# Two-layer graph network on one core: a cell's products with x computed during the pass over adj and kept in DRAM

## The chip, the core and the metric

The kernel runs on one core of a Trainium2 chip. The metric is the device time of one execution in microseconds; lower is better. Before the change it is 1171.91 us, the median of three runs (1171.31 to 1177.44). The profile is one separate execution of the same program; its span is 1052.2 us. PE stands for TensorE, DVE for VectorE, ACT for ScalarE, POOL for GpSimd, SP for SyncE.

## The reference, cut to what matters

`x` is 2708 x 256, `adj` is a sparse 2708 x 2708 matrix, both float32. Layer 0 sends two "supports" through two gated cells; layer 1 is an attention layer over the entries of adj above 0.5. Both end in a residual and a layer norm.

```python
def _gru_cell(x, hstate, Wih, Whh, bih, bhh):
    gi = x @ Wih.T + bih
    gh = hstate @ Whh.T + bhh          # hstate is x, the layer's input
    ir, iz, inn = jnp.split(gi, 3, axis=1)
    hr, hz, hn = jnp.split(gh, 3, axis=1)
    r = jax.nn.sigmoid(ir + hr)
    z = jax.nn.sigmoid(iz + hz)
    n = jnp.tanh(inn + r * hn)
    return (1.0 - z) * n + z * hstate

# layer 0
node_support = node_adj_norm @ h                       # adj without its diagonal
edge_output = _gru_cell(node_support, h, edge_Wih, edge_Whh, edge_bih, edge_bhh)
edge_support = (sum of three attention heads over the nonzeros of adj) / 3
node_output = _gru_cell(edge_support, h, node_Wih, node_Whh, node_bih, node_bhh)
x = layernorm(x + de[:, None] * edge_output + dn[:, None] * node_output)
# layer 1: four heads over adj > 0.5, then layernorm(x + ...)
```

The products `hstate @ Whh.T` depend on x and weights alone. The products with `Wih` need the supports, and those need adj.

## The kernel before

All work is on one core, in three stages.

1. **The pass over adj.** Columns of the transposed adj are taken in six groups of up to 512 (the last has 148), each in 22 blocks of 128 rows (the last has 20). For each block ScalarE makes two masks, VectorE a maximum over 64 columns at a time, and TensorE adds up flags and attention logits. After each group, `listed` turns what was found into lists of row numbers for the gathers.
2. **Layer 0.** GpSimd gathers the listed rows of adj and of a table `T0` in DRAM; TensorE multiplies them. When the columns of a group are complete, `cells_and_norm` runs the two cells for it and writes its part of layer 1's table `T1`.
3. **Layer 1.** Rows of `T1` are gathered and multiplied in the same way.

The kernel's operations are not issued in the order of the text. A class `Plan` records them with their dependences and a rough time each, and issues them in an order of its own: each engine takes next, of what is ready, the operation with the longest chain of work after it. So the text gives the dependences and not the order.

```python
def issue(self):                                     # Plan
    ...
        if op.method == "dma_start":
            moved = max(moved, t + self.LOAD) + done - self.LOAD
            end = moved
            free[e] = max(free[e], moved - self.LOAD - self.QUEUED)
```

PSUM has eight banks of 128 x 512 float32; five rings share them:

```python
accs, dbs = banks("acc", 2), banks("db", 2)
acc_bank, db_bank = ring(accs), ring(dbs)
side, pl_bank, ls_bank = ring(banks("side", 2)), ring(banks("pl", 1)), ring(banks("ls", 1))
```

The pass, for each group `g` and block `b` (eight tiles `at`, four each of `over` and `mask`):

```python
for g, cs in enumerate(groups):
    w = width[g]
    pe, pf = acc_bank(), db_bank()
    for b in range(NB):
        ...                                          # group 0: loads of xT, small products; later: one other load
        at = tiles.tile([P, CH], F32, name="at")
        nc.sync.dma_start(at[:p, :w], adjT[b * P : b * P + p, base[g] : base[g] + w])
        over = tiles.tile([P, CH], BF16, name="over", bufs=4)
        nc.scalar.activation(over[:p, :w], at[:p, :w], AF.Sign, bias=minus_half[:p])
        ...                                          # GpSimd: the diagonal block loses its diagonal
        mask = tiles.tile([P, CH], BF16, name="mask", bufs=4)
        nc.scalar.activation(mask[:p, :w], at[:p, :w], AF.Sign)
        nc.vector.tensor_reduce(found0[...], at[...], AX.X, ALU.max, apply_absolute_value=True)
        ...
        nc.tensor.matmul(pf[:NB, :w], lhsT=only[:p, b, :], rhs=over[:p, :w], ...)
        nc.tensor.matmul(pe[:H3, :w], lhsT=u3[:p, b, :], rhs=mask[:p, :w], ...)
    logits(g, pe)                                    # copies pe on ScalarE
    flags(g, pf)                                     # reads pf on VectorE
    ...
    listed(0, *ranked[0][g])
```

The cells of a group (two cells `n`, two halves `o` of the 256 outputs, three gates; `w_h` is W_hh, `w_i` is W_ih; KD is 2):

```python
def product(gate, terms):
    pg = side()
    todo = [(wt, v, k) for wt, v in terms for k in range(KD)]
    for m, (wt, v, k) in enumerate(todo):
        nc.tensor.matmul(pg[:, :w], lhsT=wt[:, k, r0 : r0 + P], rhs=v[k], ...)
    return pg[:, :w]

r, zt, t = (gp.tile([P, CH], F32, name=f"g_{v}")[:, :w] for v in "rzt")     # two buffers each
both = ((w_h, of_x), (w_i, of_s))
nc.scalar.activation(r, product(0, both), AF.Sigmoid, bias=bias(b_s, 0))
nc.scalar.activation(zt, product(1, both), AF.Sigmoid, bias=bias(b_s, 1))
nc.vector.scalar_tensor_tensor(t, product(2, both[:1]), bias(b_h, 2), r, op0=ALU.add, op1=ALU.mult)
nc.vector.tensor_add(t, t, product(2, both[1:]))
nc.scalar.activation(t, t, AF.Tanh, bias=bias(b_i, 2))
...                                                  # VectorE: (x - t) * z + t, and the sum of the cells
```

A slower general path for inputs that don't fit the lists stands behind the fast one; it isn't taken for this input.

Of the kernel before, what the change touches and what calls it, by code (L numbers as in the profile page):

```python
# [94 lines left out]
class Plan:  # L95
# [118 lines left out]
    def issue(self):  # L214
        ops, total = self.ops, len(self.ops)
        after = [[] for _ in ops]
        for n, op in enumerate(ops):
            for k in op.deps:
                after[k].append(n)
        tail, urgent = [0.0] * total, [op.urgent for op in ops]  # L220
        for n in reversed(range(total)):
            op = ops[n]
            for m in after[n]:
                tail[n] = max(tail[n], tail[m] + (0.0 if ops[m].engine == op.engine else self.LAG))
                urgent[n] = max(urgent[n], urgent[m])
            tail[n] += op.done
        tail = [t + u for t, u in zip(tail, urgent)]
        left = [len(op.deps) for op in ops]
        start = [0.0] * total
        free = dict.fromkeys(self.ENGINES, 0.0)  # L230
        ready = {e: [] for e in self.ENGINES}
        for n, op in enumerate(ops):
            if not left[n]:
                ready[op.engine].append(n)
        moved, table = 0.0, 0
        for _ in range(total):
            t, e = min((max(free[e], min(start[n] for n in ready[e])), e) for e in self.ENGINES if ready[e])
            n = max((n for n in ready[e] if start[n] <= t), key=lambda n: (tail[n], -n))
            ready[e].remove(n)
            op = ops[n]  # L240
            busy, done = op.busy, op.done
            if op.table and op.table != table:
                busy, done, table = busy + 1.3, done + 1.3, op.table
            free[e] = t + busy
            end = t + done
            if op.method == "dma_start":
                moved = max(moved, t + self.LOAD) + done - self.LOAD
                end = moved
                free[e] = max(free[e], moved - self.LOAD - self.QUEUED)
            for call in op.calls:  # L250
                call()
            for m in after[n]:
                same = ops[m].engine == e and "dma" not in op.method
                start[m] = max(start[m], end + (0.0 if same else self.LAG))
                left[m] -= 1
                if not left[m]:
                    ready[ops[m].engine].append(m)
        return max(free.values())
# [32 lines left out]
def fast_path(ctx: ExitStack, tc: tile.TileContext, i: dict, out: bass.AP, bad: bass.AP):  # L291
# [43 lines left out]
    def ring(tiles):  # L335

        return cycle(tiles).__next__
# [13 lines left out]
    T1 = dram.tile([N, TW], F32, name="f_T1")  # L351

    TS = dram.tile([NG, HEADS1, CH], F32, name="f_TS")
    plan.pitch = {T0.tensor.name: TW, T1.tensor.name: TW, TS.tensor.name: HEADS1 * CH}


    home1 = const.tile([P, 12 * CH], F32, name="f_home1")
# [214 lines left out]
    def spread(layer, cs, rows, row, place):  # L572

        n, slots = len(cs), ROWS // rows
        T = max((TILES0, TILES1)[layer][c] for c in cs)
        lhs = lists.tile([P, NB, 2 * ROWS], BF16, name="ids")
        ids = lhs.rearrange("p b (m v k) -> p v b m k", m=slots, v=2)[:, :, :, :n]
        shape = [P, NB, n, rows]
        nc.vector.tensor_tensor(
# [112 lines left out]
    def later_kd(src, wide, name):  # L692
        t = const.tile([P, KD, wide], F32, name=name)
        later(t, src.rearrange("(k p) n -> p k n", p=P))
        return t

    for b in range(0, NF, 7):
        e = min(b + 7, NF)
        later(xn[:, b:e, :], x[b * P : e * P, :].rearrange("(b p) d -> p b d", p=P))
    if NF < NB:  # L700
        later(xn[: size[NF], NF, :], x[NF * P :, :])
    cells = []
    for cell in ("edge", "node"):
        w_i = later_kd(i[f"L0_gnn_{cell}_WihT"], 3 * D, f"f_{cell}_wi")
        w_h = later_kd(i[f"L0_gnn_{cell}_WhhT"], 3 * D, f"f_{cell}_wh")
# [75 lines left out]
    def flags(g, pf):  # L781
# [14 lines left out]
        if full < len(bl):  # L796
            p = size[last]
            nc.vector.tensor_copy(flags1[:p, :, last:], v[:p, :, full:])

    for g, cs in enumerate(groups):  # L800
        w = width[g]
        pe, pf = acc_bank(), db_bank()
        c0, nf = base[g] // W0, w // W0
        for b in range(NB):
            p = size[b]
            if g == 0 and b % GR == 0:
                load_xT(b // GR)
                projected_u(b // GR)
            elif g > 0 and loads and b % 2:
                loads.pop(0)()  # L810
            at = tiles.tile([P, CH], F32, name="at")
            nc.sync.dma_start(at[:p, :w], adjT[b * P : b * P + p, base[g] : base[g] + w])
            over = tiles.tile([P, CH], BF16, name="over", bufs=4)
            nc.scalar.activation(over[:p, :w], at[:p, :w], AF.Sign, bias=minus_half[:p])
            if b in cs:
                o = b * P - base[g]
                nc.gpsimd.tensor_mul(at[:p, o : o + p], at[:p, o : o + p], off_diag[:p, :p])
            mask = tiles.tile([P, CH], BF16, name="mask", bufs=4)
            nc.scalar.activation(mask[:p, :w], at[:p, :w], AF.Sign)
            nc.vector.tensor_reduce(  # L820
                found0[:p, c0 : c0 + nf, b], at[:p, : nf * W0].rearrange("p (c i) -> p c i", i=W0), AX.X, ALU.max,
                apply_absolute_value=True,
            )
            if nf * W0 < w:
                nc.vector.tensor_reduce(
                    found0[:p, c0 + nf : c0 + nf + 1, b], at[:p, nf * W0 : w], AX.X, ALU.max,
                    apply_absolute_value=True,
                )
            nc.tensor.matmul(
                pf[:NB, :w], lhsT=only[:p, b, :], rhs=over[:p, :w], start=(b == 0), stop=(b == last)  # L830
            )
            nc.tensor.matmul(
                pe[:H3, :w], lhsT=u3[:p, b, :], rhs=mask[:p, :w], start=(b == 0), stop=(b == last)
            )
# [151 lines left out]
    def cells_and_norm(g):  # L986
# [20 lines left out]
        for n, (w_i, w_h, b_i, b_h, b_s) in enumerate(cells):  # L1007
            of_s = [(sa, es)[n][:, o, :w] for o in range(KD)]
            for o in range(KD):

                def product(gate, terms):
                    pg = side()
                    r0 = gate * D + o * P
                    todo = [(wt, v, k) for wt, v in terms for k in range(KD)]
                    for m, (wt, v, k) in enumerate(todo):
                        nc.tensor.matmul(
                            pg[:, :w], lhsT=wt[:, k, r0 : r0 + P], rhs=v[k],
                            start=(m == 0), stop=(m == len(todo) - 1),
                        )
                    return pg[:, :w]  # L1020

                def bias(t, gate):
                    return t[:, gate * KD + o : gate * KD + o + 1]

                r, zt, t = (gp.tile([P, CH], F32, name=f"g_{v}")[:, :w] for v in "rzt")
                both = ((w_h, of_x), (w_i, of_s))
                nc.scalar.activation(r, product(0, both), AF.Sigmoid, bias=bias(b_s, 0))
                nc.scalar.activation(zt, product(1, both), AF.Sigmoid, bias=bias(b_s, 1))
                nc.vector.scalar_tensor_tensor(
                    t, product(2, both[:1]), bias(b_h, 2), r, op0=ALU.add, op1=ALU.mult  # L1030
                )
# [681 lines left out]
```

## Time and profile before

| | us | share of the span | instructions |
|---|---|---|---|
| span of the profiled execution | 1052.2 | | 13904 |
| TensorE matmul busy | 859.4 | 82% | 3867 |
| VectorE busy | 658.2 | 63% | 2097 |
| GpSimd busy | 566.1 | 54% | 613 |
| TensorE weight load busy | 521.6 | 50% | 3867 |
| ScalarE busy | 505.7 | 48% | 1487 |

The DMA engines moved 106.76 MB in the span. A busy share over the whole span is a mean over the three stages, which use the engines quite differently, so the page also cuts the span into 40 equal slices and gives for each slice and engine the busy share in tenths (9 is 90% or more), the clock that TensorE was granted, and the share of the DMA engines. Groups of instructions are named by engine, operation and the tiles written and read; nearly all have the same line number, that of the class that records operations, so tiles tell them apart. The tiles of the pass have the name `f_home`, of which they are parts.

### The profile page before, as it was taken

The numbers are of one execution on the slowest core, as the hardware profiler recorded it, in microseconds if no ns is written. First come the engines' busy times: TensorE is split into PE (matmuls) and PEld (weight loads), VectorE is DVE, ScalarE is ACT, GpSimd is POOL, SyncE is SP. The second block draws the span as 40 slices with busy tenths as digits, with TensorE's granted clock in tenths as the row PEclk, the third lists the DMA queues.
The fourth block names the chain that finished last, engine by engine and source line by source line (L and its number), as shares of the span: only waits on it lengthen the run. The fifth ranks groups of instructions, "written<-read, shape, count | busy, mean of one in ns | idle before, by whom it ended". The sixth has DMA issues, their size and how long they took to land. (4 is left out here: it accounts for less than half of the span.)

```text
span 1052.2 us, 13904 instructions
## 1 busy us (share of the span) xinstructions
PE 859.4 (82%) x3867; PEld 521.6 (50%) x3867; DVE 658.2 (63%) x2097; ACT 505.7 (48%) x1487; POOL 566.1 (54%) x613
## 2 busy tenths in 40 slices
PE   4867777888779988899998989999999858768860
PEld 4423223666544446553564446446645746766650
DVE  5598698845543869624562467137525558769996
ACT  3799999676542426631473238316623420002251
POOL 2003700577877857777777777724400028787720
PEclk9986667799859989899999999999999979889985
DMA  8688985233221113221233123211300114444413
GB/s 287 184 279 250 287 252 147 52 105 88 58 71 41 35 34 90 73 72 50 66 96 116 43 68 91 62 33 53 96 0 2 49 41 112 146 126 140 112 42 109
DMA packets 71437, 106.76 MB, mean 101 GB/s; under 512 B 20792, under 2 KB 42560, under 8 KB 70712
## 3 DMA queue, kind: packets, MB, share of 16 engines
q1 hardware_dynamic: 50104, 58.63, 18.0%
q0 software_dynamic: 20320, 45.59, 16.6%
q10 hardware_dynamic: 928, 1.57, 0.4%
q8 instruction: 33, 0.54, 0.2%
q14 instruction: 52, 0.43, 0.1%
HBM read 97.21 MB, written 8.54 MB: 101 GB/s over the span
## 5 line engine op out<-in xcount | busy, mean ns | idle before, releaser
L203 POOL DMA_INDIRECT rows<-f_T,f_idx x254 | 293.7, 1156 | 217.2 <-DMA f_T<-f_home 106.4
L203 PE MATMUL acc<-four,rows 128*128 128x256 f32 (+1 forms) x712 | 202.0, 419 | 22.3 <-ACT four L203 20.0
L203 POOL DMA_INDIRECT f_home<-in_adjT_dram,f_idx x163 | 164.7, 1010 | 92.7 <-issue 32.8
L203 ACT ACTIVATE four<-four,rows 128x64 f32<-128x64 f32 (+1 forms) x534 | 145.0, 336 | 65.6 <-DMA rows<-f_T,f_idx 32.9
L203 PEld LDWEIGHTS acc<-four,rows 128*128 128x128 f32 x712 | 133.7, 202 | 58.7 <-ACT four L203 30.3
L203 DVE SCALAR_TENSOR_TENSOR f_home<-f_home,rows,f_m 128x128 f32<-128x128 f32 (+1 forms) x364 | 100.1, 343 | 27.3 <-DMA rows<-f_T,f_idx 23.2
L203 POOL DMA_INDIRECT raw<-in_adj_dram,f_idx x91 | 88.6, 974 | 29.5 <-issue 12.8
L203 ACT ACTIVATE f_home<-f_home,f_minus_half 128x512 bf16<-128x512 f32 (+3 forms) x132 | 85.6, 657 | 13.0 <-PE db L203 12.0
L203 PE MATMUL acc<-f_home,rows 128*65 128x128 f32 (+1 forms) x480 | 70.6, 304 | 21.8 <-DVE f_home L203 20.7
L203 DVE TENSOR_REDUCE f_found<-f_home 128x8 f32<-128x512 f32 (+4 forms) x154 | 76.6, 544 | 5.0 <-POOL f_home L203 4.4
L203 ACT ACTIVATE f_home<-f_home 128x512 bf16<-128x512 f32 (+2 forms) x132 | 73.4, 564 | 9.1 <-PE acc L203 6.7
L203 PE MATMUL db<-f_home,f_only 128*22 128x512 bf16 (+2 forms) x132 | 60.6, 506 | 18.8 <-ACT f_home L203 18.2
L203 PEld LDWEIGHTS acc<-f_home,rows 128*65 128x65 f32 x480 | 57.5, 152 | 32.7 <-DVE f_home L203 25.7
L203 PE MATMUL side<-f_xT,f_edge_wh 128*128 128x512 f32 (+1 forms) x144 | 65.2, 577 | 4.4 <-DVE f_home L203 4.2
L203 POOL TENSOR_TENSOR f_home<-f_home,f_off_diag 128x128 f32<-128x128 f32 (+1 forms) x22 | 11.5, 530 | 101.6 <-ACT f_home L203 88.3
L203 PE MATMUL acc<-f_home,f_home 128*9 128x512 bf16 (+2 forms) x132 | 60.5, 506 | 5.3 <-ACT f_home L203 3.6
L203 PE MATMUL side<-f_xT,f_node_wh 128*128 128x512 f32 (+1 forms) x144 | 62.3, 556 | 2.3 <-DVE f_home L203 2.3
L203 DVE SCALAR_TENSOR_TENSOR four<-f_iota,f_rel,f_home 128x64 f32<-128x64 f32 (+1 forms) x163 | 43.9, 276 | 32.0 <-DMA f_home<-in_adjT_dram,f_idx 11.7
L203 PE MATMUL side<-f_home,f_gat_w 128*128 128x512 f32 (+1 forms) x144 | 60.1, 576 | 4.2 <-DVE f_home L203 4.1
L203 PE MATMUL side<-f_home,f_node_wi 128*128 128x512 f32 (+1 forms) x144 | 62.5, 557 | 0.1
L203 DVE TENSOR_SCALAR f_m<-raw 128x128 uint8<-128x128 f32 (+1 forms) x91 | 22.0, 251 | 64.0 <-DMA raw<-in_adj_dram,f_idx 64.0
L203 PE MATMUL side<-f_home,f_edge_wi 128*128 128x512 f32 (+1 forms) x144 | 62.0, 553 | 0.0
(185 smaller groups left out, 1319.1 us busy)
## 6 DMA issues: line engine op xcount, KB each, us to landing
f_home<-in_adjT_dram SPq DMA_DIRECT2D x105, 256.0 KB, 3.4
f_home<-f_TS SPq DMA_DIRECT2D x5, 1024.0 KB
rows<-f_T SPq DMA_DIRECT2D x31, 132.0 KB, 2.4
rows<-f_T,f_idx POOLq DMA_INDIRECT x254, 2.8
f_T<-f_home SPq DMA_DIRECT2D x21, 132.0 KB, 1.7
f_xn<-in_x_dram SPq DMA_DIRECT2D x3, 896.0 KB
f_T<-f_xn SPq DMA_DIRECT2D x3, 896.0 KB, 6.5
out_dram<-f_xn SPq DMA_DIRECT2D x21, 128.0 KB, 2.0
```

The costliest lines, as they stand in the source:

```text
L203: call = lambda: f(*args, **kwargs)
```

## The change

For the first four of the six groups, the cells' products with W_hh are computed during the pass over adj and written to a DRAM tensor `XH` (48 tiles of 128 x 512 float32, 256 KB each); `cells_and_norm` reads them back. The aim is to move TensorE's work to a stage in which it has more room. To make place for it the pass handles two blocks of adj in one instruction of ScalarE and VectorE. What goes with it:

- the pass uses one pair of PSUM accumulators, and the other pair takes the kept products
- W_hh is loaded first, in group 0 of the pass
- a kept product goes through a ScalarE copy and is sent by a DMA from ScalarE's queue
- the tile `ids` of the lists has one buffer instead of two
- the planner no longer holds back engines other than sync for the DMA queue

```diff
             if op.method == "dma_start":
                 moved = max(moved, t + self.LOAD) + done - self.LOAD
                 end = moved
-                free[e] = max(free[e], moved - self.LOAD - self.QUEUED)
+                if e == "sync":
+                    free[e] = max(free[e], moved - self.LOAD - self.QUEUED)
...
+    KEPT = 4
+    XH = dram.tile([KEPT * 2 * KD * 3 * P, CH], F32, name="f_XH")
...
-        lhs = lists.tile([P, NB, 2 * ROWS], BF16, name="ids")
+        lhs = lists.tile([P, NB, 2 * ROWS], BF16, name="ids", bufs=1)
...
+    kept_bank = ring([accs[1], dbs[1]])
+    keptp = Rings(const, 2)
+    def keep(g, n, o, gate):
+        pg = kept_bank()
+        for k in range(KD):
+            nc.tensor.matmul(
+                pg[:, : width[g]], lhsT=w_hs[n][:, k, gate * D + o * P : gate * D + (o + 1) * P],
+                rhs=xT[:, k, base[g] : base[g] + width[g]], start=(k == 0), stop=(k == KD - 1),
+            )
+        t = keptp.tile([P, CH], F32, name="kept")[:, : width[g]]
+        nc.scalar.copy(t, pg[:, : width[g]])
+        nc.scalar.dma_start(place_kept(g, n, o, gate), t)
...
-        pe, pf = acc_bank(), db_bank()
+        pe, pf = accs[0], dbs[0]
-        for b in range(NB):
+        for b0 in range(0, NB, 2):
+            pair = [b0, b0 + 1]
+            at2 = tiles.tile([P, 2, CH], F32, name="at", bufs=4)
+            over2 = tiles.tile([P, 2, CH], BF16, name="over", bufs=2)
+            mask2 = tiles.tile([P, 2, CH], BF16, name="mask", bufs=2)
...
+            for _ in range(1 if g < 2 else 2):
+                if g > 0 and keeps:
+                    keep(*keeps.pop(0))
+            whole = size[b0 + 1] == P
+            if whole:
+                rows_of = adjT[b0 * P : (b0 + 2) * P, ...].rearrange("(s p) n -> p s n", p=P)
+                nc.sync.dma_start(at2[:, :, :w], rows_of)
...
+            for p, s in parts:
+                nc.scalar.activation(over2[:p, s, :w], at2[:p, s, :w], AF.Sign, bias=minus_half[:p])
...
+                nc.scalar.activation(mask2[:p, s, :w], at2[:p, s, :w], AF.Sign)
...
-                nc.scalar.activation(r, product(0, both), AF.Sigmoid, bias=bias(b_s, 0))
-                nc.scalar.activation(zt, product(1, both), AF.Sigmoid, bias=bias(b_s, 1))
-                nc.vector.scalar_tensor_tensor(
-                    t, product(2, both[:1]), bias(b_h, 2), r, op0=ALU.add, op1=ALU.mult
-                )
+                if g < KEPT:
+                    for gate, v in enumerate((r, zt, t)):
+                        nc.sync.dma_start(v, place_kept(g, n, o, gate))
+                    for gate, v in enumerate((r, zt)):
+                        nc.vector.tensor_add(v, v, product(gate, both[1:]))
+                        nc.scalar.activation(v, v, AF.Sigmoid, bias=bias(b_s, gate))
+                    of_h = t
+                else:
+                    ...                              # as before
+                nc.vector.scalar_tensor_tensor(t, of_h, bias(b_h, 2), r, op0=ALU.add, op1=ALU.mult)
```

A last pair of blocks, 128 and 20 rows, stays in two instructions.

More of the change, by code (lines that the diff above doesn't have):

```diff
@@ L353, in fast_path @@
     TS = dram.tile([NG, HEADS1, CH], F32, name="f_TS")
-    plan.pitch = {T0.tensor.name: TW, T1.tensor.name: TW, TS.tensor.name: HEADS1 * CH}
+    KEPT = 4
+    XH = dram.tile([KEPT * 2 * KD * 3 * P, CH], F32, name="f_XH")
+    plan.pitch = {XH.tensor.name: CH, T0.tensor.name: TW, T1.tensor.name: TW, TS.tensor.name: HEADS1 * CH}
     home1 = const.tile([P, 12 * CH], F32, name="f_home1")
@@ L695, in later_kd @@
         return t
+    cells = []
+    of_cells = ("edge", "node")
+    w_hs = [later_kd(i[f"L0_gnn_{cell}_WhhT"], 3 * D, f"f_{cell}_wh") for cell in of_cells]
     for b in range(0, NF, 7):
@@ L701, in fast_path @@
         later(xn[: size[NF], NF, :], x[NF * P :, :])
-    cells = []
-    for cell in ("edge", "node"):
+    for cell, w_h in zip(of_cells, w_hs):
         w_i = later_kd(i[f"L0_gnn_{cell}_WihT"], 3 * D, f"f_{cell}_wi")
-        w_h = later_kd(i[f"L0_gnn_{cell}_WhhT"], 3 * D, f"f_{cell}_wh")
         b_i = const.tile([P, 3 * KD], F32, name=f"f_{cell}_bi")
@@ L798, in flags, with place_kept @@
             nc.vector.tensor_copy(flags1[:p, :, last:], v[:p, :, full:])
+    kept_bank = ring([accs[1], dbs[1]])
+    keptp = Rings(const, 2)
+    def place_kept(g, n, o, gate):
+        at = (((g * 2 + n) * KD + o) * 3 + gate) * P
+        return XH[at : at + P, : width[g]]
+    def keep(g, n, o, gate):
[8 more added lines that the diff above has]
+        nc.scalar.dma_start(place_kept(g, n, o, gate), t)
@@ L800, in fast_path @@
+    keeps = [
+        (g, n, o, gate) for g in range(KEPT) for n in range(2) for o in range(KD) for gate in range(3)
+    ]
     for g, cs in enumerate(groups):
         w = width[g]
-        pe, pf = acc_bank(), db_bank()
+        pe, pf = accs[0], dbs[0]
         c0, nf = base[g] // W0, w // W0
-        for b in range(NB):
[L805 to L809, printed above, removed]
-                loads.pop(0)()
[L811 to L822, printed above, removed]
-            )
-            if nf * W0 < w:
@@ new lines, in fast_path @@
+        for b0 in range(0, NB, 2):
[3 more added lines that the diff above has]
+            mask2 = tiles.tile([P, 2, CH], BF16, name="mask", bufs=2)
+            for b in pair:
+                if g == 0 and b % GR == 0:
+                    load_xT(b // GR)
+                    projected_u(b // GR)
+            if loads and (g > 0 or b0 in (10, 16)):
+                loads.pop(0)()
+            for _ in range(1 if g < 2 else 2):
[3 more added lines that the diff above has]
+            if whole:
+                rows_of = adjT[b0 * P : (b0 + 2) * P, base[g] : base[g] + w].rearrange("(s p) n -> p s n", p=P)
+                nc.sync.dma_start(at2[:, :, :w], rows_of)
+            else:
+                for b in pair:
+                    nc.sync.dma_start(
+                        at2[: size[b], b - b0, :w], adjT[b * P : b * P + size[b], base[g] : base[g] + w]
+                    )
+            parts = [(P, slice(0, 2))] if whole else [(size[b], slice(b - b0, b - b0 + 1)) for b in pair]
+            for p, s in parts:
+                nc.scalar.activation(over2[:p, s, :w], at2[:p, s, :w], AF.Sign, bias=minus_half[:p])
+            for b in pair:
+                if b in cs:
+                    p, o = size[b], b * P - base[g]
+                    v = at2[:p, b - b0, o : o + p]
+                    nc.gpsimd.tensor_mul(v, v, off_diag[:p, :p])
+            for p, s in parts:
+                nc.scalar.activation(mask2[:p, s, :w], at2[:p, s, :w], AF.Sign)
+                b1, b2 = b0 + s.start, b0 + s.stop
@@ L825, in fast_path @@
                 nc.vector.tensor_reduce(
-                    found0[:p, c0 + nf : c0 + nf + 1, b], at[:p, nf * W0 : w], AX.X, ALU.max,
+                    found0[:p, c0 : c0 + nf, b1:b2].rearrange("p c b -> p b c"),
+                    at2[:p, s, : nf * W0].rearrange("p b (c i) -> p b c i", i=W0), AX.X, ALU.max,
                     apply_absolute_value=True,
                 )
-            nc.tensor.matmul(
-                pf[:NB, :w], lhsT=only[:p, b, :], rhs=over[:p, :w], start=(b == 0), stop=(b == last)
-            )
@@ L832, in fast_path @@
-            nc.tensor.matmul(
-                pe[:H3, :w], lhsT=u3[:p, b, :], rhs=mask[:p, :w], start=(b == 0), stop=(b == last)
-            )
+                if nf * W0 < w:
+                    nc.vector.tensor_reduce(
+                        found0[:p, c0 + nf : c0 + nf + 1, b1:b2].rearrange("p c b -> p b c"),
+                        at2[:p, s, nf * W0 : w].rearrange("p b (c i) -> p b c i", c=1), AX.X, ALU.max,
+                        apply_absolute_value=True,
+                    )
+            for b in pair:
+                p = size[b]
+                nc.tensor.matmul(
+                    pf[:NB, :w], lhsT=only[:p, b, :], rhs=over2[:p, b - b0, :w], start=(b == 0), stop=(b == last)
+                )
@@ L835, in fast_path @@
+            for b in pair:
+                p = size[b]
+                nc.tensor.matmul(
+                    pe[:H3, :w], lhsT=u3[:p, b, :], rhs=mask2[:p, b - b0, :w], start=(b == 0), stop=(b == last)
+                )
         logits(g, pe)
@@ L1026, in cells_and_norm @@
                 both = ((w_h, of_x), (w_i, of_s))
-                nc.scalar.activation(r, product(0, both), AF.Sigmoid, bias=bias(b_s, 0))
-                nc.scalar.activation(zt, product(1, both), AF.Sigmoid, bias=bias(b_s, 1))
-                nc.vector.scalar_tensor_tensor(
-                    t, product(2, both[:1]), bias(b_h, 2), r, op0=ALU.add, op1=ALU.mult
-                )
+                if g < KEPT:
[5 more added lines that the diff above has]
+                    of_h = t
+                else:
+                    nc.scalar.activation(r, product(0, both), AF.Sigmoid, bias=bias(b_s, 0))
+                    nc.scalar.activation(zt, product(1, both), AF.Sigmoid, bias=bias(b_s, 1))
+                    of_h = product(2, both[:1])
+                nc.vector.scalar_tensor_tensor(t, of_h, bias(b_h, 2), r, op0=ALU.add, op1=ALU.mult)
                 nc.vector.tensor_add(t, t, product(2, both[1:]))
```

## The prediction

> **What bounds the kernel now.** I read the head of the page and the 40 slices first, to cut the span into stages; then the busy time of each engine by stage; then the costliest groups; last the instructions in order of time, because a mean duration is not the spacing at which instructions of one kind follow each other.
>
> ```profile
> span 1052.2 us, 13904 instructions
> ...
> PE   4867777888779988899998989999999858768860
> ...
> DVE  5598698845543869624562467137525558769996
> ACT  3799999676542426631473238316623420002251
> ...
> PEclk9986667799859989899999999999999979889985
> DMA  8688985233221113221233123211300114444413
> ```
>
> A slice is 26.3 us. Slices 1 to 7 (to about 190 us) are the pass over adj: DMA at 8 or 9, ACT at 9, PE at 7 on a clock of only 6 to 8 tenths. Slices 8 to 32 (to about 850 us) are layer 0's gathers with the cells between them: PE at 9, DMA at 1 to 3. The last 200 us are layer 1, where DVE is highest. The busy times by stage put numbers on it (columns: PE, PEld, DVE, ACT, POOL, then granted clock, DMA share, GB/s):
>
> ```profile
> 50.00:190.00 140.00, 102.99 (x485) 41.53 (x484) 119.17 (x291) 132.09 (x261) 39.03 (x50) 0.71 0.77 233
> 190.00:338.00 148.00, 125.70 (x570) 80.77 (x571) 76.91 (x237) 82.18 (x310) 110.32 (x106) 0.86 0.28 72
> 338.00:800.00 462.00, 423.67 (x1518) 236.46 (x1517) 247.82 (x733) 203.22 (x678) 292.30 (x289) 0.96 0.24 62
> 850.00:1052.00 202.00, 131.26 (x956) 108.99 (x956) 160.35 (x657) 41.53 (x143) 116.94 (x91) 0.83 0.36 106
> ```
>
> The pass is bound by **ScalarE**: 132 of 140 us (94%), with DVE at 85% and DMA at 77% close behind. The cells' stage is bound by **TensorE**: 424 of 462 us (92%) at an almost full clock, everything else at 63% or less. The change takes work from the second and puts it into the first. I start at 50 us because before that the first group waits for TensorE's small products with the attention vectors.
>
> **What the Trainium skill says.** "ScalarE: Activation LUTs", section "What ACT_TABLE_LOAD costs": an ACTIVATE with a bias operand takes about 280 + 0.833 N ns, one without 186 + 0.833 N ns, and back-to-back ones overlap by about 93 ns. The trace agrees: the biased Sign of 512 columns takes 708 ns, the other 615 ns, those of 148 columns 403 and 309 ns, so 0.84 ns a column. "TensorE: Matmul & The Clock Gate", section "Part 1: The HAM clock gate": the clock is cut when the array is little used and released by activity. The trace fits: clock 0.71 in the pass, 0.96 in the cells. So more matmuls in the pass should raise its clock. "DMA: Bandwidth & Descriptors", section "Issuing engines are not separate DMA queues": transfers from the scalar queue run on the same 16 engines as those from sync. No run yet shows the two side by side under load; I take it as it stands.
>
> **The change, part by part.** (1) **Out of the cells' stage.** For groups 0 to 3 the products with W_h are no longer computed there. Per group: 2 cells x 2 halves x 3 gates x 2 k = 24 matmuls of the code. The trace has 120 records of 128x512 per weight for five full groups, 24 per weight and group, so each float32 matmul is two records. Their spacing:
>
> ```profile
> 575.35 1.88 PE L203 MATMUL side<-f_xT,f_edge_wh 128*128 128x512 f32 x4
> ...
> 577.07 1.88 PE L203 MATMUL side<-f_home,f_edge_wi 128*128 128x512 f32 x4
> ```
>
> Four records in 1.88 us, 0.47 us each. 48 records x 0.47 = 22.6 us a group, 90 us for four. Of that I count on 78 us (87%): PE is 92% busy there, and with its work smaller the next bounds begin to show. GpSimd is the nearest: in the stretch of 200 to 745 us it issues 155 gathers of rows at 1.09 us, 133 of adj at 1.01 and 91 for layer 1's masks at 0.97, each with about 0.3 us between them, some 510 of 545 us. The 91 mask gathers (about 115 us) can move behind, where it now waits 106 us for layer 1's table, so I don't make it the bound, but it will cost part of the gain.
>
> (2) **Into the cells' stage.** 48 loads of 256 KB, 12.6 MB, against a DMA share of 0.24: hidden if issued early enough. 32 additions on DVE at 0.68 us (the present addition of a PSUM bank to 512 columns takes 681 ns) are 22 us on an engine that is 54% busy: hidden in throughput, but each gate's chain is longer by one step. I charge nothing beyond the 13% above.
>
> (3) **Into the pass, ScalarE.** 48 copies of PSUM to SBUF. A copy of this kind takes 586 ns and, overlapping its neighbour by 93 ns as the Signs do, holds the engine for 0.49 us. After each comes a DMA issue on ScalarE's own queue, which has to wait for that copy. The trace has two issues there:
>
> ```profile
> 0.74 0.48 ACTq L203 DMA_DIRECT2D f_gat_w<-in_L_gnn_gat_W_dram  x1
> ...
> 1.26 0.59 ACTq L203 DMA_DIRECT2D f_home<-in_L_gnn_gat_a_dram  x1
> ```
>
> I take 0.48 us, as time in which no ACTIVATE starts. 48 x (0.49 + 0.48) = 47 us.
>
> (4) **Out of the pass, ScalarE.** Two blocks an instruction. The Signs now follow each other like this:
>
> ```profile
> 109.81 0.70 ACT L203 ACTIVATE f_home<-f_home,f_minus_half 128x512 bf16<-128x512 f32 x1
> ...
> 110.42 0.61 ACT L203 ACTIVATE f_home<-f_home 128x512 bf16<-128x512 f32 x1
> ...
> 110.94 0.70 ACT L203 ACTIVATE f_home<-f_home,f_minus_half 128x512 bf16<-128x512 f32 x1
> ```
>
> 0.61 and 0.52 us from start to start, of which 512 x 0.84 = 0.43 us are columns. Joining two saves 0.18 and 0.09, 0.27 us a pair, not the 0.46 us that the durations would suggest. From 50 us on there are 50 joined pairs (10 in each of five groups; the last pair of a group, with the block of 20 rows, stays apart): 14 us.
>
> (5) **Into the pass, TensorE and DMA.** The same 192 records are 90 us of PE at a full clock. PE's 103 us in the stage are largely slow matmuls: the bf16 ones take 556 ns as recorded at the low clock. PE goes to about full, but at a higher clock; its bound comes near ScalarE's. DMA: 233 GB/s at a share of 0.77 is 303 GB/s at full share. 12.6 MB less the 1.6 MB of W_h, which load earlier now, is 36 us at that rate, against 32 us of free share in the stage: just fits, with no slack.
>
> (6) **Small ones.** One accumulator pair instead of two: at each of five group ends the next group's matmuls wait for the copy (0.57 us) and the flags (0.73 us). One buffer of ids instead of two makes the lists wait for each other. 4 us together, my choice. The DVE reductions by pairs save some 0.14 us each, 7 us on an engine that is not the bound. The scheduler change only lets scalar issues go out without being held back.
>
> **Sum.** Pass: +47 - 14 = +33 us, of which the 8 us in which ScalarE is idle now could take some; but three engines near full don't mesh, so I take +38, and +4 for the small ones. Cells: -78. Together **-36 us**. The timed runs take 1171.9 us where the profiled execution spans 1052.2; the profile doesn't tell where these 120 us are, so I carry the difference over unchanged: 1171.9 - 36 = 1136 us.
>
> **Rivals.** *The pass becomes jammed.* With the writes, ScalarE, PE, DMA and DVE are all above 85%, and the four buffers of two blocks give coarser grain than eight of one. If PE or the DMA queue sets the pace the pass grows by 70 us instead of 42, and the gain is about 8 us. For it: DMA 0.77 and ACT 94% now; a kept product must pass all four. Against: kept work may wait, as nothing needs it before the gathers start using the two banks again. *The cells' stage gives back less.* GpSimd's 510 of 545 us, or loads behind others in the one sync queue, hold it: the 90 us become 45, net about 0. Against: a PE wait on gathered rows is hardly to be seen now. *Issues on ScalarE are free*, running under the next ACTIVATE: 23 us less in the pass, net about -60 us. Against: the copy has to finish before its issue. *The time outside the profile is a slower TensorE*: then the cells' stage gives more and the pass, by then bound by PE, takes more; net similar.
>
> **Range and chances.** The first two rivals bound the slow side: about +8 us if both came by half. The third with the full 90 us gives -75. So 1098 to 1180 holds it 8 times in 10. A gain of over 2% needs 23.4 us, 13 less than my centre with a spread of some 30: 0.62. Slower by over 2% needs both rivals whole: 0.07.
>
> **What would show it.** W_h's matmuls: 192 records of full width before about 235 us; after it only the 48 of group 4 and the 48 narrow ones of group 5. Layer 0's first row gather starts near 235 us where it started near 198. The clock in the pass rises from 0.71 to 0.85 or more. ScalarE stays at 90% or more in the pass, with gaps of about 0.5 us before or after each kept copy. Cells' stage: PE still at 88% or more, and the stretch from the first row gather to the last cells about 570 us instead of 650. Layer 1's last stretch stays at about 200 us. I am wrong if ScalarE is idle in the pass waiting for PE or DMA, if PE in the cells' stage falls to 80% with GpSimd or the loads as what it waits for, or if the pass isn't longer at all.

## The result, and the profile after

The changed kernel takes **1130.06 us** (median of 4, 1127.26 to 1137.39) against 1171.61 us: a ratio of 0.9646, 95% interval 0.9589 to 0.9704. The forecast was 1136 us. On another chip (e9) the ratio was 0.952 (0.945 to 0.960), so kernels that did not run side by side are compared below to about 1%, no closer. The runs e1 to e4, e5 to e8 and e9 to e12 are each from one chip, where the kernel before took 1189, 1173 and 1196 us. Medians are of all executions of a kernel, ratios only of those within 1.5% of its fastest.

The head and the slices of the changed kernel's page, a slice now being 28.4 us:

```profile
span 1135.6 us, 13859 instructions
...
PE   6986788897886678678777797887849877687860
...
DVE  5584748733454539562564285276415646688995
ACT  4686677864565425464355245335411430002251
...
PEclk9997988998887699688888888988979988879985
DMA  8687777663332213423352252232312013443513
```

Compared with the page of before, DMA stays high for nine slices (256 us) instead of seven (184 us), ScalarE is no longer at 9 in them, and TensorE, which stood at 8 to 9 in the cells' stage, is mostly at 7 to 8. The last difference is hardly the change's doing, as the next profile shows.

The span, 1135.6 us, agrees with the timed runs. That of before, 1052.2 us, had not. So the kernel before was profiled once more (e1): 1172.6 us this time. **The profile that the prediction was read from was an unusual execution**, and comparisons by stage below are with the second one, unless the first is named. In e1, too, TensorE is mostly at 6 to 9 in the cells' stage:

```profile
PE   5875566796666879696878598869899877776870
```

The marks between the stages: GpSimd's first gather of rows of `T0` (end of the pass) and the last write to `T1` (end of the cells' stage). The summary by tile gives a group's first and last start; here both groups, of before (e1), then of after:

```profile
L203 POOL DMA_INDIRECT rows<-f_T,f_idx x254: 941/947/5202, 209.2 to 1128.7; - x127
...
L203 SPq DMA_DIRECT2D f_T<-f_home x22: 294/320/372, 501.0 to 973.8; - x22
```

```profile
L203 POOL DMA_INDIRECT rows<-f_T,f_idx x254: 943/949/5805, 249.4 to 1090.7; - x127
...
L203 SPq DMA_DIRECT2D f_T<-f_home x22: 294/320/383, 506.9 to 935.0; - x22
```

And the busy times by stage (PE, PEld, DVE, ACT, POOL, then clock, DMA share, GB/s), first of before (e1), then of after:

```profile
50.00:209.00 159.00, 103.96 (x502) 44.96 (x501) 120.50 (x300) 132.29 (x268) 40.11 (x51) 0.66 0.67 198
209.00:974.00 765.00, 619.10 (x2295) 361.81 (x2294) 352.59 (x1061) 307.20 (x1038) 399.49 (x393) 0.88 0.20 53
```

```profile
50.00:249.00 199.00, 165.95 (x714) 70.24 (x715) 135.98 (x276) 147.60 (x221) 41.10 (x52) 0.91 0.73 219
249.00:935.00 686.00, 540.68 (x2082) 327.54 (x2081) 348.90 (x1051) 305.48 (x1033) 405.70 (x393) 0.86 0.30 79
```

The pass is 40 us longer (249.4 less 209.2). The cells' stage is 79 us shorter (686 against 765) and TensorE is busy for 78 us less in it (541 against 619). Layer 1 takes 199 us before and 201 after. 40 - 79 + 2 = -37 us, which is the difference of the two spans.

### The profile page after: what moved, and what is told of

Read it like the earlier page. It is cut to its first block, busy times and chain, and to the rows that moved or that the text cites. A ratio compares the mean times of both kernels' runs of the same rounds, so it can differ in the third digit from the quotient of the medians.

```text
span 1135.6 us, 13859 instructions
## 1 busy us (share of the span) xinstructions
PE 873.9 (77%) x3867; PEld 533.2 (47%) x3867; DVE 668.5 (59%) x2059; ACT 516.2 (45%) x1413; POOL 569.4 (50%) x613
## 5 line engine op out<-in xcount | busy, mean ns | idle before, releaser
L203 PE MATMUL acc<-four,rows 128*128 128x256 f32 (+1 forms) x712 | 221.3, 449 | 27.8 <-ACT four L203 21.8
L203 PEld LDWEIGHTS acc<-four,rows 128*128 128x128 f32 x712 | 146.7, 221 | 65.0 <-ACT four L203 26.1
L203 DVE TENSOR_REDUCE f_found<-f_home 128x16 f32<-128x1024 f32 (+5 forms) x84 | 71.4, 883 | 13.6 <-DMA f_home<-in_adjT_dram 8.1
L203 ACT ACTIVATE f_home<-f_home,f_minus_half 128x1024 bf16<-128x1024 f32 (+4 forms) x72 | 69.7, 977 | 21.4 <-PE side L203 6.8
L203 DVE TENSOR_TENSOR f_home<-f_home,side 128x512 f32<-128x512 f32 (+1 forms) x56 | 36.8, 657 | 63.1 <-remote 20.8
L203 ACT ACTIVATE f_home<-f_home 128x1024 bf16<-128x1024 f32 (+4 forms) x72 | 62.6, 880 | 20.2 <-PE acc L203 16.2
L203 PE MATMUL db<-f_home,rows 128*65 128x128 f32 x376 | 54.2, 299 | 12.3 <-DVE f_home L203 9.1
L203 ACT COPY f_home<-acc 128x128 f32<-128x128 f32 (+5 forms) x61 | 20.8, 343 | 92.1 <-PE acc L203 57.9
L203 ACT ACTIVATE m<-four 128x64 bf16<-128x64 f32 (+1 forms) x181 | 40.3, 246 | 48.0 <-PE acc L203 13.9
L203 PE MATMUL db<-f_home,f_only 128*22 128x512 bf16 (+2 forms) x132 | 42.5, 407 | 20.0 <-ACT f_home L203 17.4
```

Of the source, the lines that this page charges most:

```text
L203: call = lambda: f(*args, **kwargs)
```

## The experiments

**e1: the kernel before, again.** No edit.

> The kernel before, unchanged, with a new profile. The changed kernel's profiled span (1135.6 us) equals its timed runs, while that of the kernel before (1052.2 us) lies 118 us under its timed runs. If that one profile was an unusual execution, this one spans about 1168 to 1172 us, and the missing 118 us can be located by stage: I expect most of them in the cells' stage (about 750 us instead of 650). If the profiler itself shortens this kernel, the span is again near 1052 us.

1186.2 us beside 1189.2 for the same program on that chip, ratio 0.996 (0.993 to 1.000): so a ratio within half a percent of 1 says nothing here. The profiled span was 1172.6 us: the first was unusual, the profiler doesn't shorten the kernel. That first execution was itself timed, at 1054.1 us, so its span of 1052.2 us is real. By stage, from the first profile to the second: pass 197 to 209 us, cells' stage 662 to 765, layer 1 193 to 199. In e1, engines stand still together, once in the pass and often in the cells' stage. Instructions of e1 in order of time, ScalarE's, with what ended the idle time before them in brackets ("remote" is a release that the profile doesn't show the origin of):

```profile
126.53 0.72 ACT L203 ACTIVATE f_home<-f_home,f_minus_half 20x512 bf16<-20x512 f32 x1 [17.58 <-remote]
...
370.81 0.59 ACT L203 COPY f_home<-side 128x512 f32<-128x512 f32 x1 [14.24 <-remote]
...
541.90 0.69 ACT L203 ACTIVATE f_home<-side,f_edge_bs 128x512 f32<-128x512 f32 x1 [12.52 <-remote]
...
674.21 0.69 ACT L203 ACTIVATE f_home<-side,f_edge_bs 128x512 f32<-128x512 f32 x1 [14.03 <-remote]
```

Of ScalarE's stops of over 3 us with "remote" or "issue" as releaser there are 14 in e1, 112 us together: 17.6 us in the pass, 87.5 us (12 of them) in the cells' stage, 7.0 us in layer 1. The first profile has one, of 4.5 us. In the stops that I followed, VectorE, TensorE and sync soon stand too, while GpSimd goes on issuing gathers back to back.

**e2: two blocks an instruction, nothing kept.**

```diff
-    KEPT = 4
+    KEPT = 0
...
-        pe, pf = accs[0], dbs[0]
+        pe, pf = acc_bank(), db_bank()
...
-        lhs = lists.tile([P, NB, 2 * ROWS], BF16, name="ids", bufs=1)
+        lhs = lists.tile([P, NB, 2 * ROWS], BF16, name="ids")
```

> Two blocks an instruction and nothing kept (W_hh still loaded first, both accumulator pairs, two ids buffers). By my sum ScalarE loses 14 us in the pass, so 1155 to 1162 us against 1171.6, ratio 0.985 to 0.993. Rival, that the joined blocks are worth little because buffers of two blocks make the grain coarser: 1168 to 1180 us. Rival, that joining is the larger part of the gain: 1135 us or less.

Ratio 0.995 (0.991 to 0.999), beside e1's 0.996 on the same chip. The joining by itself brings nothing that can be told from the unchanged program. Its pass isn't shorter either: the first row gather of its profile comes at 224.4 us (209.2 in e1), which is what the rival of coarser grain would give.

**e3: kept, but not read.** The cells compute everything as before.

```diff
-                if g < KEPT:
+                if False:
```

> The changed kernel, but the cells compute all products as before and the kept ones in DRAM are not read: the pass pays and the cells gain nothing. By my sum the changed kernel's 1130 us plus 78 us: about 1208 us (ratio to before 1.03). If the cells' stage gave only half, about 1170 us; if it gave the whole 90 us or more, 1220 us or more.

1205.6 us, ratio 1.016 (1.010 to 1.022), where 1.03 was expected. The time itself is close to the 1208 of the sum only because this chip is slower; on the chip of the result the ratio means 1190 us. Keeping costs and joining gives back less: +16 us against the median of before. One thing was not expected, and has the size of what is missing: the first row gather comes at 231 us, not 249, with the same products. Copies of kept products by stage, until the first row gather and after it, in the changed kernel and in e3 (ScalarE's busy us and count):

```profile
50.00:249.00 199.00, 23.33 (x41) 0.91 0.73 219
249.00:330.00 81.00, 4.06 (x7) 0.85 0.36 100
```

```profile
50.00:231.00 181.00, 22.02 (x39) 0.92 0.75 225
231.00:330.00 99.00, 4.07 (x7) 0.88 0.32 92
```

With two more before 50 us, e3 too has 41 copies ahead of its first gather, in a pass 18 us shorter. The work of keeping is the same; what differs is the planner's order, in which a product that the cells wait for has a longer chain behind it and goes ahead of work of the pass. That the order makes the 18 us is my reading of one profile each; no run changed the order alone.

**e4: a quarter kept, all read.** Twelve products are kept, those of group 0, and groups 1 to 3 read them too in place of their own.

```diff
-        at = (((g * 2 + n) * KD + o) * 3 + gate) * P
+        at = ((n * KD + o) * 3 + gate) * P
...
-        (g, n, o, gate) for g in range(KEPT) for n in range(2) for o in range(KD) for gate in range(3)
+        (g, n, o, gate) for g in range(1) for n in range(2) for o in range(KD) for gate in range(3)
```

> The changed kernel with 12 products kept (group 0) instead of 48, and all four groups read those 12, so groups 1 to 3 work with group 0's values. The cells gain as in the changed kernel, the pass pays a quarter of the keeping. By my sum the keeping costs 47 us of ScalarE's time, of which three quarters go: 35 us less than the changed kernel, about 1095 us. If keeping is hidden in the pass, no change: about 1128 us. If PE or DMA were jammed: 1080 us or less.

1101.7 us, the median of four that scatter from 1083 to 1121 us; ratio 0.919 (0.911 to 0.928). From e3 to e4, on one chip, it is -104 us by the medians and -117 us by the executions that the ratios count: the cells' gain, and three quarters of the keeping. It says that keeping 36 more products is not hidden. What they cost is known only roughly: by the ratios 39 us (beside e9's 0.952) to 53 us (beside 0.965), by the medians from different chips 28 us. So it doesn't decide between the 35 us expected and the rival "jammed". The first row gather of its profile comes at 220.8 us, 29 us before the changed kernel's.

**e5: keeping with one block an instruction.** The pass's loop of before, with eight buffers of one block, and the keeping of the change in it.

```diff
-        for b0 in range(0, NB, 2):
-            pair = [b0, b0 + 1]
-            at2 = tiles.tile([P, 2, CH], F32, name="at", bufs=4)
+        for b in range(NB):
 ...
+            if b % 2 == 0:
+                for _ in range(1 if g < 2 else 2):
+                    if g > 0 and keeps:
+                        keep(*keeps.pop(0))
+            at = tiles.tile([P, CH], F32, name="at")
 ...                                          # the rest of the loop as in the kernel before
```

> The changed kernel with one block an instruction in the pass (eight buffers of one block, as before), keeping and reading as in the change. By my sum the joining saves 14 us of ScalarE's time in a pass that it bounds, so this is 10 to 15 us slower than the changed kernel: ratio to before 0.975. But the changed kernel's trace has ScalarE busy for only 102 of 140 us in the pass, with the loads of adj waiting for VectorE to give back buffers. If the coarse buffers are what holds the pass, this is no slower or faster than the changed kernel: 0.955 to 0.965.

Ratio 0.958 (0.949 to 0.966), where 0.975 was expected and the rival had 0.955 to 0.965. Not slower than the change; by these intervals it can't be called faster either. ScalarE is busy for 11 us more in a pass that ends at the same time (first row gather at 250.6 us):

```profile
50.00:251.00 201.00, 167.78 (x707) 66.66 (x707) 134.37 (x343) 158.78 (x316) 41.52 (x52) 0.86 0.71 212
```

ScalarE's time is saved by the joining, as forecast (147.6 us in the changed kernel, 158.8 here), and the pass gets no shorter by it. Two readings are left: ScalarE isn't what the pass waits for, or its 11 us are lost again to buffers of two blocks instead of one, which the joining brings with it. No run changed one without the other.

**e6 and e7: without the 91 gathers of layer 1's masks**, in the kernel before and in the changed one. Every mask is made from one loaded tile, so layer 1 works with other masks.

```diff
-        r = small.tile([P, W1], F32, name="raw1", bufs=6)
-        gathered(r[:, :w], adj, idx1[:, c, m : m + 1], d0)
+        r = one_raw
```

> The kernel before without the 91 gathers of layer 1's masks (all masks are made from one loaded tile; the rows of layer 1 and all else as before). In the second profile of the kernel before, ScalarE stands still 13 times for 3 to 18 us, 112 us in all, each time while GpSimd issues gathers back to back, and with no releaser that the profile shows; the first profile, 118 us shorter, has one such stop. If the stops come from GpSimd's runs of gathers, fewer gathers mean fewer stops: 1080 to 1120 us, ratio 0.92 to 0.955. If they have nothing to do with GpSimd, the gathers are off the path and it stays at 1160 to 1172 us.

> The changed kernel without the 91 mask gathers. With e6 this tells whether the change's 41 us come from TensorE's work in the cells' stage, or from fewer stops (69 us of stops of ScalarE in the changed kernel's profile against 112). If from TensorE's work, this is 35 to 45 us faster than e6. If from stops, it is within 15 us of e6.

1120.5 and 1067.8 us, ratios 0.956 (0.949 to 0.962) and 0.913 (0.907 to 0.919). The gathers of the masks cost the kernel before some 50 us, though nothing waits for their data until layer 1. It is the cells' stage that is shorter without them; here that of e6, then of e7, columns as above:

```profile
214.00:921.00 707.00, 606.25 (x2295) 357.54 (x2295) 349.15 (x1061) 306.74 (x1038) 315.35 (x302) 0.90 0.20 49
```

```profile
244.00:864.00 620.00, 521.45 (x2077) 317.42 (x2076) 337.18 (x986) 304.49 (x1033) 320.51 (x301) 0.90 0.29 76
```

That is 707 us instead of 765 and 620 instead of 686. The change is worth 52.6 us here, more than the 35 to 45 expected. The stops (14 in e1 by the count above, not 13) are 65 us in e6 (8 of them) and 29 us in e7 (6), so by this pair alone fewer stops could be part of the gain; e9 and e12 rule that out.

**e8: five groups kept.**

```diff
-    KEPT = 4
+    KEPT = 5
```

> Five groups kept instead of four (60 products). Against a run with 12 written, 36 products more lengthen the time to the first row gather by 28 us, 9 us a group of 12, and the cells' stage is shorter by 79 us for four groups, 20 us each. So a fifth group should bring some 10 us: ratio to before 0.955. If kept products delay the second pair of accumulators further, no gain or a loss: 0.965 to 0.98.

Ratio 0.954 (0.947 to 0.961). In the direction expected, but within what the changed kernel itself gave on two chips (0.965 and 0.952).

**e9: the changed kernel, again.** No edit.

> The changed kernel, unchanged, beside the other three on the same chip: ratio to before 0.96 to 0.97. In its profile the first row gather comes at 245 to 255 us, the cells' stage takes 670 to 700 us; ScalarE's long stops with no releaser add up to 50 to 90 us again, as in its first profile, if their number belongs to the program and not to chance.

1139.5 us beside 1195.9, ratio 0.952 (0.945 to 0.960), a little more than expected. First row gather at 247.9 us, cells' stage 692 us: the stages repeat within 6 us. The stops don't: 19, 113 us together, more than the 50 to 90 expected, where the first profile of this kernel had 10 and 69 us, for spans that differ by 7 us. The sum of ScalarE's stops therefore doesn't add to the time one for one, and I draw no number from it. It also shows that the gain isn't one of fewer stops: with 113 us of them the span is 1142.2 us, where e1 with 112 us had 1172.6 on a chip that is, if anything, the faster one.

**e10 and e11: one block an instruction, five and six groups kept.**

```diff
-    KEPT = 4
+    KEPT = 5                                 # e10; 6 in e11
```

> One block an instruction as in e5 and five groups kept as in e8. e5 stood at 0.9576 and e8 at 0.9538 where the change stood at 0.9646; if the two gains add, 0.947. If the pass is held by the keeping as such, so that the finer buffers matter less when more is kept, 0.955.

> All six groups kept. The sixth is 148 columns wide: 24 matmul records of each cell at about 0.17 us, so at most 8 us less in the cells' stage, and 12 more copies, issues and loads of short rows. 0 to 5 us either way of e10.

e10: 1128.1 us (1121.4 to 1134.2), ratio 0.945 (0.936 to 0.954). It has the lowest ratio of the versions that compute everything, by less than the intervals (e8 0.954, e5 0.958); beside it on the same chip the changed kernel took 1139.5 us (1136.4 to 1144.0), and the two ranges don't meet, though the intervals of the ratios do. e11: 1145.5 us, 0.956 (0.948 to 0.965): the narrow group is not worth keeping. It takes 17 us more than e10, where 5 at most had been expected; its first row gather comes at 276.5 us, 20 us after e10's. Why the last twelve products cost so much wasn't tried.

**e12: the products left out.** The kernel before without W_hh's products in groups 0 to 3: no keeping, no reading, no additions; the third gate uses x in their place.

```diff
-                both = ((w_h, of_x), (w_i, of_s))
+                both = ((w_i, of_s),) if g < 4 else ((w_h, of_x), (w_i, of_s))
...
-                    t, product(2, both[:1]), bias(b_h, 2), r, op0=ALU.add, op1=ALU.mult
+                    t, of_x[o] if g < 4 else product(2, both[:1]), bias(b_h, 2), r, op0=ALU.add, op1=ALU.mult
...
-                nc.vector.tensor_add(t, t, product(2, both[1:]))
+                nc.vector.tensor_add(t, t, product(2, ((w_i, of_s),)))
```

> The kernel before, with the W_hh products of groups 0 to 3 left out altogether: no keeping, no loads, no additions (the gates lack those terms, and the third uses x in their place). It measures by itself what TensorE's 90 us are worth in the cells' stage: by the prediction's 87%, 78 us, so 1095 us, ratio 0.934, with the first row gather where it was before. If GpSimd or another engine takes over, 45 us: 0.962. If stops also become fewer, 0.92.

1098.3 us, ratio 0.916 (0.906 to 0.925): some 100 us under before on that chip. First row gather at 208.0 us, as in the kernel before. The cells' stage by busy times, as above:

```profile
208.00:896.00 688.00, 540.98 (x2097) 329.58 (x2096) 346.25 (x1056) 306.75 (x1037) 401.66 (x393) 0.86 0.24 59
```

TensorE is busy for 541 us, 78 less than in e1 and the same as in the changed kernel. The stage ends at 895.6 us, so it takes 688 us, 77 less than in e1, and the changed kernel's on the same chip (e9) 692. The ratio is lower than the 0.934 expected; 0.92 had been given for the case of fewer stops, but stops are not fewer: 22, 130 us together. So the loads of 12.6 MB and the 32 additions take next to nothing, and all that separates the changed kernel from e12, 1139.5 against 1098.3 us, is 41 us, of which the first row gather shows 40. Of e9, then of e12:

```profile
L203 POOL DMA_INDIRECT rows<-f_T,f_idx x254: 940/946/7042, 247.9 to 1097.8; - x127
```

```profile
L203 POOL DMA_INDIRECT rows<-f_T,f_idx x254: 940/946/5991, 208.0 to 1054.0; - x127
```

It is **the price of keeping, with all that goes with it, paid in the pass.**

## Why the prediction was right, and where it was not

**The cells' stage, -78 us: right, from a sum that was off.** Measured 79 us by stage (e1 to the changed kernel). But the two lines that the sum was read from start at 575.35 and 577.07 us: four records take 1.72 us from start to start and not 1.88, which makes 0.43 us each and 83 us for the 192, not 90. Of these 83 us, 95% came back; the share of 87% was too cautious and made up for it. By time e12 gives even 101 us (interval 90 to 112), more than the work that was left out; by stage, against e1, it gives 77. The kernel before has no profile from e12's chip, so that difference stays open. The argument for the 87% had a weak leg, too: TensorE at 92% of that stage was a feature of the unusual execution. In e1 it is 619 of 765 us, 81%, and its work still comes back almost in full. My reading, which no run tests by itself, is that most of the stage's idle time of TensorE lies in stretches in which it could not have worked, not in slack that other work hides.

**Loads and additions hidden: right**, shown by e9 against e12. **GpSimd as the next bound: it did not hold this gain back**, but its gathers do cost time: leaving out 91 of them shortened the stage by 58 us before and 66 after (e6 and e7). TensorE is busy for 79% of the changed stage, where 88% had been named; in e1 it was 81%, so the change did not bring that about.

**The pass, +42 us: near in size, for a partly wrong reason.** By e1 the pass is 40 us longer. But ScalarE stands still for 17.6 us in e1's pass (13.4 us in e12's), and for 3.6 us in the changed kernel's (10.4 us in e9's). Against the first profile, which has no such stop and is the one that the forecast was read from, the pass is 53 us longer (249.4 less 196.8). So the price lies between 40 and 53 us, and that 42 is so near the lower end is in part luck. The step that failed is "the pass is bound by ScalarE, so these terms are its length". ScalarE is busy for 147.6 of 199 us, 74%, where I had said 90% or more, and of its 51 idle us about half are waits for TensorE, which I had named as a sign of being wrong. ScalarE's waits in the changed kernel from 50 to 249 us (us in all, times, longest):

```profile
ACT ids L203 <- DVE ids L203: 11.3, 8, 5.4
ACT f_home L203 <- PE side L203: 6.8, 1, 6.8
ACT f_home L203 <- PE acc L203: 6.6, 6, 2.9
ACT f_home L203 <- PE db L203: 6.2, 9, 1.2
ACT got L203 <- PE pl L203: 5.0, 3, 2.9
```

In e1's pass it waits for TensorE for 1.7 us. Nothing is full in the changed pass: TensorE 83%, DMA 0.73. From 190 us on, where 18 of the 41 copies lie (all 48 had been forecast ahead of the first gather), TensorE is the fullest:

```profile
190.00:249.00 59.00, 53.65 (x220) 22.93 (x215) 41.54 (x99) 45.40 (x86) 7.56 (x12) 0.97 0.64 179
```

91% there. The loads of adj, meanwhile, wait for VectorE to give back a buffer (the sync queue's waits from 50 to 249 us):

```profile
SPq L203 <- DVE f_found L203: 92.9, 31, 9.4
SPq L203 <- ACT f_home L203: 32.4, 26, 5.6
```

That wait isn't new, it is 64.6 us in e1's pass; and in e5, whose pass is as long, it is 38.1 us and the wait for ScalarE 78.6. So no one wait sets the length. My reading is that the pass is a loop of several engines with few buffers in which each kept product takes a place; the rival "jammed" was nearer to that than my main line, though it forecast 70 us. How the 40 to 53 us divide between TensorE, the order of the plan (18 us by e3, one profile) and the buffers stays open.

The terms themselves: a kept product was to hold ScalarE for 0.97 us. It does where the issue comes right behind its copy; ScalarE's instructions of the changed kernel in order of time:

```profile
127.80 0.56 ACT L203 COPY kept<-db 128x512 f32<-128x512 f32 x1
128.39 0.33 ACTq L203 DMA_DIRECT2D f_XH<-kept  x1
128.82 1.15 ACT L203 ACTIVATE f_home<-f_home,f_minus_half 128x1024 bf16<-128x1024 f32 x1 [0.46 <-ACT kept L203]
```

That is 1.02 us to the next ACTIVATE, and 0.96 to 1.05 us in 19 other cases of the 48; the issue takes 0.33 us, not 0.48. But in 14 cases the plan had put another instruction between the copy and its issue:

```profile
80.47 0.56 ACT L203 COPY kept<-db 128x512 f32<-128x512 f32 x1
80.94 1.15 ACT L203 ACTIVATE f_home<-f_home,f_minus_half 128x1024 bf16<-128x1024 f32 x1
81.06 0.33 ACTq L203 DMA_DIRECT2D f_XH<-kept  x1
81.99 1.04 ACT L203 ACTIVATE f_home<-f_home 128x1024 bf16<-128x1024 f32 x1
```

There the next ACTIVATE starts 0.47 us after the copy, and the one after it 1.05 us later, as it does without an issue (1.06 us from 128.82 to 129.88). So the rival of free issues was right for these: what costs is the wait for the copy to end, not the issue. The joining was to save 14 us of ScalarE's time and saved 11 (e5).

**The clock: right.** 0.66 in the pass before (e1), 0.91 after, where 0.85 or more was forecast. It agrees with what the Trainium skill says in "TensorE: Matmul & The Clock Gate", section "Part 1: The HAM clock gate": activity of the array releases the throttle on its clock.

**The time outside the profile: carried over, which was the luck of it.** The 120 us were not outside at all: 103 of them lie in the cells' stage (662 against 765 us). I had offered a slower TensorE as their place; its clock is lower (0.845 against 0.888 over the span), but its busy time is only 24 us longer (883 against 859). The visible difference is the stops. That the change is worth as much in either kind of execution could not be known, and isn't shown: there is no unusual execution of the changed kernel, and with fewer stops (e6 and e7) it was worth 53 us. The forecast of a stage of 570 us (686 measured) was off for this reason. That of the first row gather, 235 us against 249.4, was not: there the pass was reckoned too short, and its own +42 us would have put the mark at 240. One more sum was loose: the first two rivals by half give about -5 us, not +8.

## What to carry to other kernels

Moving work out of the stage that TensorE bounds paid nearly its full busy time back here, though TensorE looked only 81% busy. What it cost in the other stage was not to be had from a sum on the engine that looked fullest, so measure the two halves by themselves: the work left out (e12), and the work done but not used (e3). Where ScalarE sends on what it has just copied, put another instruction between the copy and the issue; in the 14 cases above that kept about half a us of ScalarE's time each. Before a prediction is read from a profile, compare its span with the timed runs; if they differ by a tenth, the profile shows another execution than the one to be improved, and a second profile is the first thing to take.

## What was not expected of the hardware

The same program spanned 1052.2 us in one profiled execution and 1172.6 in another, while all other timed executions of it lay at 1164 us and above. In e1, TensorE, VectorE, ScalarE and sync stand still together, for 15.6 us in the longest such stretch that I followed (110.9 to 126.5 us), while GpSimd issues gathers back to back at one per 1.25 us (until 122.8 us here), and the profile names no releaser. Taking 91 of the gathers away, whose results are not needed until layer 1, took about 50 us off the time. That may be a sign that the runs of gathers have a part in the stops; but the gathers of rows also queue behind them on GpSimd, which would cost time without any stop. What holds the engines was not found.
